# A graph layer on one core: in 13 of 128 edge blocks the last 128 source rows are fetched one by one by SyncE

## The chip, the cores and the metric

The kernel runs on one core of one Trainium2 chip. The metric is the device time of one execution in microseconds (us), median of several runs. An execution is also recorded by the hardware profiler, and all rows below come from that one recorded execution. TensorE is called PE, VectorE DVE, ScalarE ACT, GpSimd POOL and SyncE SP; PEld is the loading of weights into PE, which overlaps with its matmuls.

## The reference, cut to what matters

There are N = 8192 nodes with C = 256 numbers each, and E = 131072 edges, sorted by their destination. For every edge a message is made from the source node's row and 64 numbers of the edge; messages are summed by destination. Beside this runs attention inside groups of 32 nodes, and both results go through dense layers and a layer norm.

```python
ea = edge_attr @ w_e + b_e
msg = jax.nn.relu(x[src] + ea)
agg = jax.ops.segment_sum(msg, dst, num_segments=N)
t = x + agg
h_local = jax.nn.relu(t @ w1 + b1) @ w2 + b2
...
qkv = hd @ in_w.T + in_b
...
out = h_local + h_attn
out = out + (jax.nn.relu(out @ m_w1 + m_b1) @ m_w2 + m_b2)
...
x = _layernorm(x + ..., axis=-1)
```

The part that matters here is `x[src]`: 131072 rows of 1 KB that are picked by an index.

## The kernel before, in words

**Blocks.** The edges are cut into 128 blocks of 1024. In a block an edge has a place (h, j, partition) with h of 4, j of 2 and 128 partitions, so a block's source rows fill a tile `xs` of 128 partitions by 8 rows of 256 numbers (8 KB in each partition). `gather(b)` (lines 131 to 143) fills it with eight indirect DMAs on POOL (line 138), each with 128 indices, one row for each partition. The indices of the first two blocks come from `srcd`, later ones from `srci`. The rows come from `x` in the first 20 blocks (`NX`) and later from `xb`, a copy of `x` in DRAM to which the bias `b_e` has been added. `xs` has five buffers: the gather of block b can start when DVE has read the buffer of block b - 5. A gather is put into the program two blocks ahead of its use, but since POOL does little else, it runs as early as the buffers let it.

**A block's steps.** `load_edges(b)` (line 151) loads the block's 256 KB of edge numbers on SP's queue into one of two buffers `ea`. `edge_transpose` (line 162, DVE) turns it to `eaT` and thereby frees `ea`; the next load waits for that. `edge_products` (line 181, PE) multiplies `eaT` by `we` into two PSUM tiles `pe`; in the first 20 blocks a matmul with `sel` and `be` adds the bias (line 175). `edge_messages` adds `pe` and `xs` on DVE in two halves (line 201), and ACT applies the relu (line 202). `edge_sums` (line 221, PE) sums the messages within windows, ACT copies the sums out, `edge_place` (line 239, PE) places them among the nodes, and DVE adds them to the node tile `xT` (line 249). When all blocks of a chunk of 512 nodes are placed, the chunk's dense layers (line 496) may run.

**Order of the work.** PE's order is fixed when the program is made. Up to block 104 (`TAIL`) a loop goes through pairs of blocks and lets `work.run` put so many microseconds of attention and dense work ("fill") between the steps of a pair, by a fixed allowance. From block 104 on a planner takes over. It keeps a clock `t` and a table `came`, in which the rows of block i are due at 11.5 + 10.06 (i + 1) us; it starts at `came[102]` + 24, places a block's messages no earlier than `came`, and puts fill into the gaps as long as there is any that may run. In this part each block's messages also stand behind the newest addition to `xT` in DVE's queue. The last piece of fill is the dense work of the last 128 nodes, which needs the last block.

**SP's queue** carries the loads of `ea` and of node tiles (`xn`, line 255), the copies for `xb` (lines 566 and 572), and the output (line 549). The queue is in order: what stands behind a waiting DMA waits too. The program gives every SP DMA one of eight semaphores in turn, and each one waits until the DMA eight before it has landed.

Of the kernel before, what the change touches and what calls it, by code (L numbers as in the profile page):

```python
# [9 lines left out]
FP = mybir.dt.float32  # L10
I32 = mybir.dt.int32
# [7 lines left out]
P = 128  # L19
N, C, E, ED, H, NPG = 8192, 256, 131072, 64, 4, 32  # L20
DH = C // H
KC = C // P
BE = 1024
NB = E // BE
NH = 4
WN = P // NH
TJ = BE // NH // P
TB = NH * TJ
QR = 32
# [7 lines left out]
TN = CH // P  # L37
# [6 lines left out]
TE = 8  # L44
RS = 1.0 / (1.0 + 1e-5) ** 0.5
LN_EPS = 1e-5
REST = -1.0


# [4 lines left out]
def gnn_kernel(ctx: ExitStack, tc: tile.TileContext, x, src, dst, edge_attr, w, out):  # L54
# [30 lines left out]
    agg = dram.tile([AGG_ROWS, C], FP, name="agg")  # L85

    srci = const.tile([P, NB, TB], I32, name="srci")
    rel = const.tile([P, NB, TB], FP, name="rel")
    wrow = const.tile([P, NB], FP, name="wrow")
    width = const.tile([1, 1], I32, name="width")  # L90
    we = const.tile([P, ED // QR, C], FP, name="we")
    be = const.tile([P, C], FP, name="be")
    w1 = const.tile([P, KC, C], FP, name="w1")
    w2 = const.tile([P, KC, C], FP, name="w2")
    mw1 = const.tile([P, KC, 2 * C], FP, name="mw1")
# [32 lines left out]
        return pps.tile([P, 2, CH], FP, name="pe", tag="pe", bufs=2)  # L128


    xs_of = {}

    def gather(b):
        xs = epool.tile([P, NH, TJ, C], FP, name="xs", tag="xs", bufs=5)
        for h in range(NH):
            for j in range(TJ):
                idx = srcd[:, b * NH + h, j : j + 1] if b < ND else srci[:, b, h * TJ + j : h * TJ + j + 1]
                nc.gpsimd.indirect_dma_start(  # L138
                    out=xs[:, h, j, :],
                    out_offset=None,  # L140
                    in_=x if b < NX else xb[:, :],
                    in_offset=bass.IndirectOffsetOnAxis(ap=idx, axis=0),
                )
        xs_of[b] = xs
# [3 lines left out]
    def load_edges(b):  # L148

        ea = ea_of[b] = epool.tile([P, BE // P * ED], FP, name="ea", tag="ea", bufs=2)  # L150
        nc.sync.dma_start(ea, edge_attr[b * BE : (b + 1) * BE, :].rearrange("(p q) d -> p (q d)", p=P))

    gather(0)
    gather(1)
# [7 lines left out]
        nc.vector.transpose(eaT, ea.rearrange("p (m t d) -> p t m d", m=EQ, d=QR))  # L162


    pe_of, msg_of, oh_of, newest = {}, {}, {}, {}

    def edge_products(b):

        eaT = eaT_of.pop(b).rearrange("p t m r -> p t (m r)")
        pes = [bank2().rearrange("p i (j c) -> p i j c", j=TJ) for _ in range(2)]  # L170
        pe_of[b, 0], pe_of[b, 2] = pes
        quarter = [slice(h * QR, (h + 1) * QR) for h in range(NH)]
        if b < NX:
            for h, rows in enumerate(quarter):
                nc.tensor.matmul(  # L175
                    pes[h // 2][:, h % 2], sel[rows, :], be[rows, None, :].to_broadcast([QR, TJ, C]), start=True, stop=False, skip_group_check=True
                )
        for j in range(TJ):
            for i in range(ED // QR):
                for h, rows in enumerate(quarter):  # L180
                    nc.tensor.matmul(  # L181
                        pes[h // 2][:, h % 2, j, :], eaT[rows, j * ED // QR + i, :], we[rows, i, :],
                        start=(b >= NX and i == 0), stop=(i == 1), skip_group_check=True,
                    )

    def next_edges(b):
        if b < NB:
            edge_transpose(b)
        if b + 2 < NB:
            load_edges(b + 2)  # L190

    def edge_messages(b):

        xs = xs_of.pop(b)
        msg = msg_of[b] = epool.tile([P, NH, TJ, C], FP, name="msg", tag="msg", bufs=3)
        n = 2 if b < NB - 1 else 1
        for h in range(0, NH, 2):
            pe = pe_of.pop((b, h))
            for u in range(0, 2, n):
                hs = slice(h + u, h + u + n)  # L200
                nc.vector.tensor_add(msg[:, hs], pe[:, u : u + n], xs[:, hs])  # L201
                nc.scalar.activation(msg[:, hs], msg[:, hs], AF.Relu)  # L202

    def edge_hot(b):
# [52 lines left out]
    with tc.tile_pool(name="setup", bufs=1) as sp:  # L257
# [7 lines left out]
        for h in range(NH):  # L265
            nc.sync.dma_start(we[h * QR : (h + 1) * QR], w["w_e"].rearrange("(i d) c -> d i c", d=QR))
        load_edges(1)
        nc.sync.dma_start(be, w["b_e"][None, :].to_broadcast([P, C]))
        nc.sync.dma_start(dsti_r, dst.rearrange("(s e) -> s e", s=NB))
        in_r = npool.tile([P, 3 * KC, C], FP, name="in_r", tag="m1")  # L270
        out_r = npool.tile([P, KC, C], FP, name="out_r", tag="vn")
# [9 lines left out]
        for h in range(NH):  # L281
            nc.vector.tensor_copy(
                srcf[:, h * TJ : (h + 1) * TJ],
                srci_r[:, h * BE // NH : (h + 1) * BE // NH].rearrange("s (r m j) -> s j m r", r=QR, m=EQ),
            )
        for h in range(NH):
            ps = bank()[:, : TJ * NB].rearrange("p (j s) -> p j s", j=TJ)
            for j in range(TJ):
                nc.tensor.transpose(ps[:, j, :], srcf[:, h * TJ + j].rearrange("s m r -> s (m r)"), ident)
            nc.vector.tensor_copy(srci[:, :, h * TJ : (h + 1) * TJ].rearrange("p s j -> p j s"), ps)  # L290
# [277 lines left out]
    def copy_store(i):  # L568
        for _, c, n in steps[i] if 0 <= i < len(steps) else []:
            xp = xp_of.pop(c)  # L570
            nc.vector.tensor_add(xp, xp, be[:, None, :].to_broadcast([P, n * TN, C]))
            nc.sync.dma_start(rows(xb, c, n), xp)

    class Work:
# [64 lines left out]
    with tc.manual_schedule(engines={PE}):  # L639
# [70 lines left out]
            b += 2  # L710
        work.calm = True

        came = [11.5 + 10.06 * (i + 1) for i in range(NB)]
        t, p, m, s, l = came[b - 2] + 24, b, b, b - 2, b - 2
        added = dict((i, came[i] + 2.0) for i in range(b))
        summed_at, bank_free = {}, t
# [168 lines left out]
```

## Time and profile before

| | |
|---|---|
| median of 3 runs | 1327.83 us (1325.05 to 1328.84) |
| the profiled execution | 1328.6 us, of which its span is 1326.8 us |
| PE busy | 1210.8 us (91%), granted clock 0.961 on average |
| POOL busy | 981.7 us (74%), 1024 gathers |
| DVE busy | 784.8 us (59%) |
| ACT busy | 587.8 us (44%) |
| HBM traffic | 155 GB/s over the span |

The span lies 1.8 us under the execution's own time, and that execution lies 0.8 us above the median. Busy shares are averages over all stages. POOL's share needs care: a gather is recorded with about 0.95 us and followed by 0.30 us in which the next one is issued, and this pattern goes on without a break, so that a POOL which is 74% busy has in fact no time left. An idle time is put down to the event that came last; `issue` means that none is seen.

### The profile page before, as it was taken

Reading aid. Unit: us, or ns where it says so; the run is one execution under the profiler, and the core shown is the slowest. Engines: PE = TensorE matmul, PEld = TensorE weight load, DVE = VectorE, ACT = ScalarE, POOL = GpSimd, SP = SyncE. Lnnn points to the kernel's source line nnn. Section 1 sums busy time; section 2 is a strip of 40 time slices with the busy share of each in tenths; the row PEclk is TensorE's granted clock in tenths of the full one; section 3 lists DMA queues with packets and bytes.
Section 4 is the critical chain, followed back from the end, with each engine's and each line's share of the span. In section 5 each row is a group of like instructions: output and inputs, shape, how many; then the busy total and the mean of one; then the engine's idle time right before and its main releaser. Section 6 shows DMA issues by size and latency. Waiting matters only on the chain.

```text
span 1326.8 us, 24218 instructions
## 1 busy us (share of the span) xinstructions
PE 1210.8 (91%) x9683; PEld 738.3 (56%) x9683; DVE 784.8 (59%) x1347; ACT 587.8 (44%) x842; POOL 981.7 (74%) x1032
## 2 busy tenths in 40 slices
PE   5998899999999889898998989899999999989887
PEld 3565555555555556555564555555555565545655
DVE  6566655747565555745566474655558475565654
ACT  2534344444545354453535444444454545344433
POOL 7777777777777777777777777777777777777770
PEclk7998999999998899999899989999999999989999
DMA  8877554545454544545454454544545445444541
GB/s 284 274 253 272 189 174 136 167 130 160 137 169 128 162 129 131 160 136 163 129 146 143 135 160 131 160 139 129 162 137 170 129 139 160 131 143 130 161 122 32
DMA packets 92754, 207.10 MB, mean 156 GB/s; under 512 B 20798, under 2 KB 39644, under 8 KB 91868
## 3 DMA queue, kind: packets, MB, share of 16 engines
q0 software_dynamic: 49152, 134.28, 34.6%
q1 hardware_dynamic: 42908, 71.20, 16.3%
q8 instruction: 78, 1.28, 0.4%
q14 instruction: 40, 0.33, 0.1%
q10 hardware_dynamic: 576, 0.00, 0.0%
HBM read 188.64 MB, written 16.78 MB: 155 GB/s over the span
## 4 chain that ended last, share of the span: by engine, by line
PE 34%; POOL 30%; issue 16%; DVE 10%; DMA 6%; ACT 4%; SPq 1%; DVEq 0%; ACTq 0%; POOLq 0%
POOL xs L138 30%; PE at L496 10%; PE pe L181 8%; DMA xs<-xb,srci 4%; DVE msg L201 4%; PE at L399 4%; PE pw L221 3%; PE l L239 2%; PE at L477 2%; PE at L413 1%; ACT pr L440 1%; DVE eaT L162 1%; PE pe L175 1%; ACT msg L202 1%; PE at L465 1%
## 5 line engine op out<-in xcount | busy, mean ns | idle before, releaser
L138 POOL DMA_INDIRECT xs<-xb,srci x864 | 821.4, 951 | 263.1 <-issue 250.1
L202 ACT ACTIVATE msg<-msg 128x1024 f32<-128x1024 f32 (+1 forms) x258 | 270.0, 1050 | 443.2 <-DVE msg L201 440.3
L201 DVE TENSOR_TENSOR msg<-pe,xs 128x1024 f32<-128x1024 f32 (+1 forms) x258 | 305.0, 1196 | 157.3 <-PE pe L181 121.1
L181 PE MATMUL pe<-we,eaT 32*128 32x256 f32 x4096 | 297.8, 409 | 29.3 <-DVE msg L201 26.5
L181 PEld LDWEIGHTS pe<-we,eaT 32*128 32x128 f32 x4096 | 225.7, 197 | 122.2 <-issue 68.6
L138 POOL DMA_INDIRECT xs<-in_x_dram,srci x144 | 143.2, 995 | 43.9 <-issue 41.7
L162 DVE STREAM_TRANSPOSE eaT<-ea 128x512 f32<-128x512 f32 x128 | 90.2, 704 | 103.7 <-PE pe L181 98.3
L221 PE MATMUL pw<-msg,oh 128*32 128x256 f32 x2048 | 128.6, 386 | 1.6 <-DVE xT L249 1.6
L496 PE MATMUL at<-hA,mw 128*128 128x512 f32 (+2 forms) x304 | 122.6, 534 | 4.0 <-DVE hA L506 3.9
L496 PE MATMUL at<-m,mw 128*128 128x512 f32 (+2 forms) x304 | 119.4, 533 | 7.0 <-ACT m L512 6.5
L399 PE MATMUL at<-xT,inT 128*128 128x512 f32 x256 | 120.8, 599 | 0.3 <-ACT xT L389 0.2
L239 PE MATMUL l<-oh,ws 128*128 128x160 f32 x512 | 93.5, 323 | 4.6 <-ACT ws L227 3.6
L221 PEld LDWEIGHTS pw<-msg,oh 128*32 128x32 f32 x2048 | 59.2, 110 | 63.6 <-issue 24.5
L239 PEld LDWEIGHTS l<-oh,ws 128*128 128x128 f32 x512 | 76.4, 198 | 31.5 <-issue 23.5
L496 PE MATMUL at<-xT,w 128*128 128x512 f32 (+2 forms) x152 | 68.8, 586 | 23.9 <-DVE xT L249 22.9
L496 PEld LDWEIGHTS at<-m,mw 128*128 128x128 f32 x304 | 54.1, 191 | 57.5 <-issue 44.2
L496 PEld LDWEIGHTS at<-hA,mw 128*128 128x128 f32 x304 | 52.9, 190 | 53.5 <-issue 39.7
L399 PEld LDWEIGHTS at<-xT,inT 128*128 128x128 f32 x256 | 46.7, 190 | 54.3 <-issue 47.8
L496 PE MATMUL at<-h,w 128*128 128x512 f32 (+2 forms) x152 | 62.8, 537 | 2.8 <-ACT h L503 2.7
L521 DVE SCALAR_TENSOR_TENSOR zT<-at,s,zT 128x512 f32<-128x512 f32 (+2 forms) x38 | 25.3, 666 | 66.8 <-PE at L496 66.2
L477 PE MATMUL at<-oT,outT 128*128 128x512 f32 x128 | 62.2, 613 | 1.9 <-ACT oT L472 1.9
L413 PE MATMUL at<-inT,xT 128*128 128x256 f32 x256 | 60.7, 384 | 2.8 <-ACT qk L402 2.8
(107 smaller groups left out, 1143.9 us busy)
## 6 DMA issues: line engine op xcount, KB each, us to landing
ea<-in_edge_attr_dram SPq DMA_DIRECT2D x128, 256.0 KB
xs<-xb,srci POOLq DMA_INDIRECT x864
xn<-in_x_dram SPq DMA_DIRECT2D x16, 512.0 KB
out_dram<-y SPq DMA_DIRECT2D x14, 512.0 KB
xp<-in_x_dram SPq DMA_DIRECT2D x10, 512.0 KB
xb<-xp SPq DMA_DIRECT2D x10, 512.0 KB
xp<-in_x_dram SPq DMA_DIRECT2D x3, 1024.0 KB
xb<-xp SPq DMA_DIRECT2D x3, 1024.0 KB
```

What stands on the lines that cost most here:

```text
L138: nc.gpsimd.indirect_dma_start(out=xs[:, h, j, :], out_offset=None, in_=x if b < NX else xb[:, :], in_offset=bass.IndirectOffsetOnAxis(ap= ...
L162: nc.vector.transpose(eaT, ea.rearrange("p (m t d) -> p t m d", m=EQ, d=QR))
L181: nc.tensor.matmul(pes[h // 2][:, h % 2, j, :], eaT[rows, j * ED // QR + i, :], we[rows, i, :], start=(b >= NX and i == 0), stop=(i == 1), ...
L201: nc.vector.tensor_add(msg[:, hs], pe[:, u : u + n], xs[:, hs])
L202: nc.scalar.activation(msg[:, hs], msg[:, hs], AF.Relu)
L221: nc.tensor.matmul(pw[h * WN : (h + 1) * WN, i, :], oh[:, h * TJ + j, :], msg[:, h, j, :], start=(j == 0), stop=(j == TJ - 1), skip_group_ ...
L239: nc.tensor.matmul(l2[:, k, i * NPB : i * NPB + WB], ws[:, i, k * P : (k + 1) * P], oh2[:, i, :], start=(i == 0 and k == 0), stop=(i == la ...
L399: nc.tensor.matmul(ps, inT[:, k, o * P : (o + 1) * P], xT[:, k, :], start=(k == 0), stop=(k == KC - 1))
L413: nc.tensor.matmul(ps[:, (t - t0) * C : (t - t0 + 1) * C], xT[:, k, t * P : (t + 1) * P], inT[:, k, 2 * C :], start=(k == 0), stop=(k == K ...
L477: nc.tensor.matmul(ps, outT[:, k, o * P : (o + 1) * P], oT[:, k, :], start=(k == 0), stop=(k == KC - 1))
L496: nc.tensor.matmul(ps, wt[:, k, o * P : (o + 1) * P], act[:, k, :], start=(k == 0), stop=(k == nk - 1))
L521: nc.vector.scalar_tensor_tensor(zT[:, o, :], layer(mw2, 2 * KC, o, m1), s3[:, o : o + 1], zT[:, o, :], op0=ALU.mult, op1=ALU.add)
```

## The change

Blocks 31, 39, ..., 127 (13 blocks, `R0` = 31, `RB` = 8) gather only seven of their eight index columns. Their last 128 rows go into a tile `xr` of 1 KB in each partition (two buffers). They are fetched in eight portions of 16, one portion in each of the eight blocks ahead: `load_rows(b)` is called at the end of `next_edges`, right after the load of `ea`; SP loads 16 indices from the tile `srcr` into registers, and then issues 16 DMAs of one row each, with the address from a register. `tc.issue_after` keeps them behind the newest load of `ea`. The tile `srcr` is a copy of the indices of the last column, made once at the start. Where a block has such rows, the second addition of `edge_messages` is split in two, 768 and 256 numbers wide, the second one reading `xr`.

Room for this is made in SBUF: `xs` has four buffers, not five. The bias tile `be` grows from 1 KB to 2 KB in each partition, and is loaded already repeated. The planner's table `came` counts 1.2575 us for a gather (eight of them are 10.06 us) and leaves out those that are gone.

```diff
+RB = 8
+R0 = 31
...
+    srcr = const.tile([P, P], I32, name="srcr")
...
-    be = const.tile([P, C], FP, name="be")
+    be = const.tile([P, TJ, C], FP, name="be")
...
+    by_row = range(R0, NB, RB)
+
+    def load_rows(b):
+
+        q = next((q for q in by_row if b < q), None)
+        if q is None or b < q - RB:
+            return
+        if q not in xr_of:
+            xr_of[q] = epool.tile([P, C], FP, name="xr", tag="xr", bufs=2)
+        p0, p1 = ((b - q + RB + k) * P // RB for k in range(2))
+        _, rows = nc.values_load_multi_w_load_instructions(
+            srcr[q : q + 1, p0:p1], engines=(mybir.EngineType.SP,), min_val=0, max_val=N - 1,
+            skip_runtime_bounds_check_because="indices of nodes",
+        )
+        with tc.issue_after(newest["ea"]):
+            for p, row in enumerate(rows, p0):
+                nc.sync.dma_start(xr_of[q][p : p + 1, :], (x if q < NX else xb)[ds(row, 1), :])
...
-        xs = epool.tile([P, NH, TJ, C], FP, name="xs", tag="xs", bufs=5)
+        xs = epool.tile([P, NH, TJ, C], FP, name="xs", tag="xs", bufs=4)
         for h in range(NH):
-            for j in range(TJ):
+            for j in range(TJ - (b in by_row and h == NH - 1)):
...
-        nc.sync.dma_start(ea, edge_attr[b * BE : (b + 1) * BE, :].rearrange("(p q) d -> p (q d)", p=P))
+        newest["ea"] = nc.sync.dma_start(ea, edge_attr[b * BE : (b + 1) * BE, :].rearrange("(p q) d -> p (q d)", p=P)).ins
...
             load_edges(b + 2)
+        load_rows(b)
...
-                nc.vector.tensor_add(msg[:, hs], pe[:, u : u + n], xs[:, hs])
+                by = (msg[:, hs], pe[:, u : u + n], xs[:, hs])
+                if b in by_row and hs.stop == NH:
+                    a, p, g = (t.rearrange("p h j c -> p (h j) c") for t in by)
+                    k = a.shape[1] - 1
+                    nc.vector.tensor_add(a[:, :k], p[:, :k], g[:, :k])
+                    nc.vector.tensor_add(a[:, k], p[:, k], xr_of.pop(b))
+                else:
+                    nc.vector.tensor_add(*by)
...
-        nc.sync.dma_start(be, w["b_e"][None, :].to_broadcast([P, C]))
+        nc.sync.dma_start(be, w["b_e"][None, None, :].to_broadcast([P, TJ, C]))
...
+        nc.vector.tensor_copy(srcr, srcf[:, TB - 1].rearrange("s m r -> s (m r)"))
...
-        came = [11.5 + 10.06 * (i + 1) for i in range(NB)]
+        came = [11.5 + 1.2575 * ((i + 1) * TB - sum(q <= i for q in by_row)) for i in range(NB)]
```

More of the change, by code (lines that the diff above doesn't have):

```diff
@@ L128, in bank2 @@
         return pps.tile([P, 2, CH], FP, name="pe", tag="pe", bufs=2)
-    xs_of = {}
+    xs_of, newest = {}, {}
+    xr_of = {}
+    by_row = range(R0, NB, RB)
[13 more added lines that the diff above has]
+                nc.sync.dma_start(xr_of[q][p : p + 1, :], (x if q < NX else xb)[ds(row, 1), :])
     def gather(b):
-        xs = epool.tile([P, NH, TJ, C], FP, name="xs", tag="xs", bufs=5)
+        xs = epool.tile([P, NH, TJ, C], FP, name="xs", tag="xs", bufs=4)
         for h in range(NH):
-            for j in range(TJ):
+            for j in range(TJ - (b in by_row and h == NH - 1)):
                 idx = srcd[:, b * NH + h, j : j + 1] if b < ND else srci[:, b, h * TJ + j : h * TJ + j + 1]
@@ L162, in edge_transpose @@
         nc.vector.transpose(eaT, ea.rearrange("p (m t d) -> p t m d", m=EQ, d=QR))
-    pe_of, msg_of, oh_of, newest = {}, {}, {}, {}
+    pe_of, msg_of, oh_of = {}, {}, {}
     def edge_products(b):
@@ L175, in edge_products @@
                 nc.tensor.matmul(
-                    pes[h // 2][:, h % 2], sel[rows, :], be[rows, None, :].to_broadcast([QR, TJ, C]), start=True, stop=False, skip_group_check=True
+                    pes[h // 2][:, h % 2], sel[rows, :], be[rows], start=True, stop=False, skip_group_check=True
                 )
@@ L570, in copy_store @@
             xp = xp_of.pop(c)
-            nc.vector.tensor_add(xp, xp, be[:, None, :].to_broadcast([P, n * TN, C]))
+            nc.vector.tensor_add(xp, xp, be[:, 0:1, :].to_broadcast([P, n * TN, C]))
             nc.sync.dma_start(rows(xb, c, n), xp)
```

## The prediction

> **What bounds the kernel now.** I read the page's engine shares and its chain first, then the waits, then POOL's and DVE's timelines side by side. The page's chain names POOL:
>
> ```profile
> PE 34%; POOL 30%; issue 16%; DVE 10%; DMA 6%; ACT 4%; SPq 1%; DVEq 0%; ACTq 0%; POOLq 0%
> L138 POOL DMA_INDIRECT xs<-xb,srci x864 | 821.4, 951 | 263.1 <-issue 250.1
> ```
>
> The gathers are one unbroken row: POOL's timeline shows 0.95 us each and 0.30 us to the next, the same at 452 us and at 1224 us:
>
> ```profile
> 452.42 0.95 POOL L138 DMA_INDIRECT xs<-xb,srci  x1 [0.30 <-issue]
> ...
> 734.91 0.94 POOL L138 DMA_INDIRECT xs<-xb,srci  x1 [0.30 <-issue]
> ...
> 1225.30 0.95 POOL L138 DMA_INDIRECT xs<-xb,srci  x1 [0.30 <-issue]
> ...
> 1295.42 0.94 POOL L138 DMA_INDIRECT xs<-xb,srci  x1 [0.30 <-issue]
> ```
>
> 1024 of 1.25 us are 1280 us, and the last one ends at 1296.4. So POOL has no slack, and it never waited for a buffer. But does anyone wait for POOL? The chain cannot tell, because it steps back along POOL's own queue. I laid each block's two additions (L201) beside its eight gathers (POOL's timeline counted in eights). From block 46 on, the first addition begins 3.8 to 19.0 us after the block's last gather has ended, in blocks 60 to 103 mostly 10 to 15. A gather lands some 2.7 to 3.7 us after its end (chain rows "694.11 2.74 DMA xs" and "755.20 3.67"). Among blocks 26 to 126 I find DVE idle for a gather in three places alone, blocks 35, 37 and 43, with 0.89, 0.17 and 1.88 us. DVE's timeline, two of them, and block 120, whose last gather is the 1225.30 row above (ended 1226.25):
>
> ```profile
> 374.89 1.23 DVE L201 TENSOR_TENSOR msg<-pe,xs 128x1024 f32<-128x1024 f32 x1 [0.89 <-DMA xs<-xb,srci]
> ...
> 456.51 1.23 DVE L201 TENSOR_TENSOR msg<-pe,xs 128x1024 f32<-128x1024 f32 x1 [1.88 <-DMA xs<-xb,srci]
> ...
> 1237.81 1.22 DVE L201 TENSOR_TENSOR msg<-pe,xs 128x1024 f32<-128x1024 f32 x1
> ```
>
> Who does end DVE's waits is in the list of waits: PE's products, not gathers (other rows put down to gathers, as at 820.7, come 18 us after the gather in question had ended, so their cause was another):
>
> ```profile
> DVE msg L201 <- PE pe L181: 121.1, 49, 9.0
> ...
> DVE msg L201 <- DMA xs<-xb,srci: 14.3, 8, 4.7
> ...
> SPq L151 <- DVE eaT L162: 962.1, 117, 21.7
> ```
>
> So PE, 91% busy in an order written out beforehand, sets the pace; POOL runs at nearly the same pace, ahead of it. SP mostly waits.
>
> **The change part by part.**
>
> *Gathers removed.* 13 x 1.25 = 16.3 us of POOL's row. On the path lies only what somebody waited for: 0.89 + 0.17 + 1.88 = 2.9 us. Blocks 31 and 39 bring gathers 1.25 us forward before block 35, and 2.5 before block 43, more than these waits. PE felt the largest: it was idle for 4.21 us before 457.95 (a dense layer waiting for `xT`, which stood behind that addition). Bounds: 0 (the next wait takes its place) to 16.3. I take -2.9, by the DVE rows. In blocks 46 to 103 nothing is taken: PE's order is the same there and its fill allowance is too, so the cover is PE's own work; if the cover were gone, the full 16.3 would show.
>
> *The tail, from block 104.* The planner's due times shrink by 1.2575 us at 103, 111, 119 and 127, so from its start to the last block by 5.0 us: fill of that size leaves the early tail and stands later. Whether that is a gain depends on idle PE later. Between 1200 and 1300 us PE was busy 86.38 of 100 us, so 13.6 idle, mostly around blocks with no fill (products waiting for the additions to free PSUM). All 5.0 may fall into it, or none. I take -4, nearer to the idle side since 13.6 is well over 5.0.
>
> *Four buffers.* The gather of block b now waits for the addition of block b - 4. In the profile the smallest distance between that addition's end and the gather's start is 9.0 us (the addition of block 68 ends at 725.9, the gather of block 72 starts at 734.9), 9.4 at block 80, 9.3 at block 100, else mostly 12 to 25. POOL's advance by then is 7.5, 8.8 and 11.3 us: it is stopped for about 2 us at block 100 if PE is unmoved. Nothing waits for these gathers, which are still some 20 us ahead of use, so the cost is 0; the cover is that lead.
>
> *SP.* In 104 block steps (8 for each of 13 blocks) come one index load, 16 register steps and 16 DMAs. Price of a row's DMA: this trace has issues of small transfers at the start (`vec_r`), 0.23 to 0.30 us each:
>
> ```profile
> 7.08 0.60 SPq L275 DMA_DIRECT2D vec_r<-in_L_gnn_b_dram  x2
> 7.86 0.23 SPq L275 DMA_DIRECT2D vec_r<-in_L_gnn_bn_g_dram  x1
> ...
> 14.12 0.40 SPq L276 DMA_DIRECT2D in_r<-in_L_gnn_in_w_dram  x1
> ```
>
> Lower bound 0.23 us; upper bound with waits for the eighth before, 12 issues from 7.08 to 14.12, or 0.59 each (DMA then 89% busy, now 45 to 55%). A register step is not in the trace: between SP's shortest event (0.017 us) and one more issue (0.23). I take 0.30 for the row, nearest to the plain issue. The index load: the nearest is the wait at the program's end for such a load (L763, up to 0.5 us). Together 16 x 0.30 + 0.5 + 0.33 for `ea` = 5.6 us of each 10.06; if the second eight rows wait for the first to land (2.7 to 3.7 us), 6 to 7. SP is moved past nothing that can't bear it: `ea` loads were issued 10.0 us (block 108) or, mostly, 16 to 25 us ahead of their transposes; `xn` of chunk 13 was issued 10.8 us ahead of PE's use, the tightest, and a batch in front of it takes at most some 5 us of that. Cost 0, upper bound in the rival below.
>
> The Trainium skill's page "DMA: Bandwidth & Descriptors", "Anatomy of one DMA — SWDGE (gpsimd) path", gives about 2.0 us fixed for a DMA, however small. This speaks against 16 single rows, and agrees with the 2.7 us landing; with eight in flight it would make 2 x 2.0 = 4 us a batch, less than SP's issue time taken above, so the sum is the same by either. The same page's "Latency and other measured facts" puts an index load at a floor of about 0.6 us, against the 0.5 taken here; an estimate from it changes a batch by 0.1.
>
> *DMA engines.* The same 1 KB rows, 16 per block beside 1024: their bytes were gathered before. Cost 0; if all rows of a batch went to one of the 16 engines, at 0.08 us a packet (q1: 16.3% of 16 x 1326.8 us over 42908 packets) that engine gets 1.3 us more per block on top of about 5.
>
> *DVE.* 13 split additions. From the row widths (1024: 1.204 us, 512: 0.660) the fixed part is 0.12 us, plus up to seven waits of 0.02 to 0.05 for the row semaphores: at most 0.5 each, 6 us in all, DVE being 59% busy. PE was seen waiting for an addition in 43 of 256 cases, so one sixth of it, +1. Bounds 0 to +6.
>
> *Start.* `be` loads 256 KB, not 128, while DMA runs at 298 GB/s: 0.4 us, and a copy of the indices on DVE, 0.2 by a row of like width. Bounds 0 to +0.6; +0.5.
>
> Sum: -2.9 - 4 + 0 + 0 + 1 + 0.5 = -5.4 us against the profiled execution's 1328.6, so 1323.2; that execution is 0.8 above the median, so **1322.4**.
>
> **The rivals.**
>
> *POOL's row does set the time.* The chain's 30% and 16% speak for it, the 3.8 to 19 us of lead against. Then 16.3 us come off less 1.5: 1327.8 - 14.8 = 1313.0.
>
> *Hidden anyway.* The three waits are followed by others, and the tail's fill only moves: -1.4 to +1.5, so 1326 to 1329. For it: between 280 and 1320 us PE was idle for only 76 us (1040 less 964.44 busy), mostly by its own chains.
>
> *SP becomes the bound.* The place is the batch behind each `ea` load, which keeps the next load, and through it the transposes and products, behind 16 rows. It decides when a row passes (10.06 - 0.33 - 0.5 - 0.1) / 16 = 0.57 us, the 0.1 being SP's other DMAs. At the upper bound of 0.59 a block takes 10.4, so 104 x 0.3 = 31 us more: 1359; each further 0.1 us costs 166. For it: the start's 0.59, and the untried register form. Against: the plain 0.23 to 0.33.
>
> *The new tail order makes PE wait.* A dense layer that stands too early waits for `xT`, as at 457.95 (4.21 us). Two such waits more, and the idle part not filled: 2 x 4.2 + 1.5 - 2.9 = +7, so 1335. It decides from one such wait more. Against: the plan keeps its own rules.
>
> **How the numbers follow.** Forecast 0.50 (1316 to 1323.8); POOL's row 0.10; hidden 0.17; SP 0.12; tail order 0.11. About 0.3%, 4 us, is what a measurement tells from no change. Faster 0.50 + 0.10 = 0.60, same 0.17, slower 0.12 + 0.11 = 0.23. The range 1313 to 1337 leaves out SP's 0.12, about half of POOL's 0.10, and little else.
>
> **What would show it.** Right: POOL's gathers end 14 to 16 us earlier, at about 1281 to 1283; additions lag them by more than 10 us in the tail; no addition waits for a gather in blocks 35, 37, 43; PE's idle between 1200 and the end falls by some 4 us; SP's rows take 0.25 to 0.35 us and its waits for `eaT` stay several us long. Wrong: DVE waiting for `ea` or `xr`, SP's row over 0.5 us, or a saving near 16 us, which would say that the lead of the gathers was not slack.

## The result, and the profile after

The changed kernel takes 1316.85 us (median of 6 runs, 1311.77 to 1319.88), the kernel before 1327.96 us (median of 6, 1325.05 to 1328.90): a ratio of 0.9916 with a 95% interval of 0.9891 to 0.9940, or 11.1 us less (8.0 to 14.5). The forecast was 1322.4, or 5.4 less. The profiled execution took 1319.52 us, with a span of 1317.7.

Two things have to be known to read the numbers below. First, a run's time moves with the clock that the throttle grants to PE, and this clock differs from run to run (0.960 to 0.976). So besides the medians I give each kernel's time at the clock 0.968, read from a straight line through all of its own runs. Second, in two of the four sessions of experiments this program was far slower on the whole, the kernel before too (2075.01 and 2030.11 us, granted clock about 0.83), so that the times of each of these two are compared within it alone.

| kernel | median us (runs) | ratio to before, 95% interval | us against before | us at clock 0.968, against before's 1326.7 |
|---|---|---|---|---|
| changed kernel | 1316.85 (6) | 0.9916 (0.9891 to 0.9940) | -11.1 | 1317.9, -8.8 |
| rows, old planner table | 1325.31 (12) | 0.9985 (0.9969 to 1.0002) | -2.0 | 1324.8, -1.9 |
| new planner table alone | 1320.58 (6) | 0.9951 (0.9933 to 0.9969) | -6.5 | 1321.6, -5.1 |
| four buffers alone | 1327.14 (12) | 1.0001 (0.9988 to 1.0014) | 0.1 | 1327.2, 0.5 |
| rows in blocks 31 and 39 alone | 1322.84 (12) | 0.9965 (0.9952 to 0.9978) | -4.6 | 1323.6, -3.1 |
| changed, rows left out | 1314.23 (4) | 0.9904 (0.9888 to 0.9921) | -12.7 | 1314.7, -12.1 |
| changed, small bias, earlier table | 1311.77 (4) | 0.9883 (0.9866 to 0.9899) | -15.5 | 1314.0, -12.7 |

The fourth column is the ratio's distance from 1 times 1328; the ratio is not quite that of the two medians. The last column says how far a kernel lies from the kernel before at the same clock.

Of the page after, the busy row, the chain and the group of the gathers:

```profile
PE 1203.5 (91%) x9683; PEld 734.1 (56%) x9683; DVE 784.9 (60%) x1361; ACT 587.5 (45%) x842; POOL 972.6 (74%) x1019
...
PE 48%; POOL 16%; DVE 11%; issue 10%; DMA 9%; ACT 5%; SPq 1%; DVEq 0%; POOLq 0%; ACTq 0%
...
L159 POOL DMA_INDIRECT xs<-xb,srci x851 | 812.3, 954 | 259.6 <-issue 245.0
```

PE's busy share is as before, but its busy time is 7.3 us less (1210.8 to 1203.5). This is hardly the change's doing: the profile of four buffers alone, a kernel that is no faster by its median, has 1204.3 (granted clock 0.967, where the profile before has 0.961 and the one after 0.966). POOL still runs without a break, 0.95 us and 0.30 us in turn, but its part of the chain has halved from 30% to 16%. The shares cannot say whether that is the gain: they walk along POOL's row as long as there is one.

The list of waits after. The columns are who waited for whom, the total in us, the number of waits and the longest:

```profile
DVE msg L230 <- PE pe L202: 123.7, 50, 10.4
...
DVE msg L230 <- DMA xs<-xb,srci: 8.9, 5, 3.1
...
PE at L418 <- DMA xn<-in_x_dram: 1.6, 1, 1.6
```

The additions wait for PE's products as before (50 waits, 123.7 us against 49, 121.1), and less for gathers (8.9 us against 14.3). Most of the waits put down to gathers are not real, before and after: laid beside the gathers from block 26 on, the additions of these waits began either 1.9 to 3.9 us after the end of the last gather that they need, or 7.7 us and more after it, and in the second case the gather had long landed. By this measure 2.9 us of the 14.3 are real, in the three blocks that the prediction names, and 1.3 us of the 8.9: 0.21 us in block 37 and 1.07 us in block 45 (at 474.95 us). One matmul group has waited 1.6 us for a node tile `xn`. SP's waits for `eaT`, in the same list for SP alone, are a quarter of the old 962.1 us:

```profile
SPq L172 <- DVE eaT L183: 241.3, 53, 13.0
```

The timelines of the changed kernel show the places where the prediction looked. Columns: start in us, length, engine, line, operation, and in brackets the idle time ahead of it with what ended it.

```profile
395.86 1.23 DVE L230 TENSOR_TENSOR msg<-pe,xs 128x1024 f32<-128x1024 f32 x1 [0.21 <-DMA xs<-xb,srci]
...
455.48 1.98 PE L526 MATMUL at<-xT,w 128*128 128x512 f32 x4 [2.08 <-DVE xT L278]
...
1258.71 0.70 PE L202 MATMUL pe<-we,eaT 32*128 32x256 f32 x4 [1.06 <-DVE msg L230]
1260.43 2.00 PE L202 MATMUL pe<-we,eaT 32*128 32x256 f32 x28 [1.03 <-DVE msg L230]
1266.50 4.91 PE L202 MATMUL pe<-we,eaT 32*128 32x256 f32 x32 [1.72 <-DVE msg L230]
...
1283.29 0.95 POOL L159 DMA_INDIRECT xs<-xb,srci  x1 [0.30 <-issue]
...
1294.92 1.88 DVE L230 TENSOR_TENSOR msg<-pe,xs 128x512 f32<-128x512 f32 x3
```

The dense layer in block 43 waits 2.08 us for `xT` where it waited 4.21. The last gather ends at 1284.2, 12.1 us earlier than before, and the last block's additions begin 10.7 us after it. In the tail the products' waits for additions are fewer. These are the waits of more than 1 us of the kernel before between 1180 and 1310 us:

```profile
1221.78 2.00 PE L181 MATMUL pe<-we,eaT 32*128 32x256 f32 x28 [1.44 <-DVE msg L201]
1239.08 0.70 PE L181 MATMUL pe<-we,eaT 32*128 32x256 f32 x4 [1.91 <-DVE msg L201]
1240.93 3.51 PE L181 MATMUL pe<-we,eaT 32*128 32x256 f32 x28 [1.15 <-DVE msg L201]
1268.12 0.70 PE L181 MATMUL pe<-we,eaT 32*128 32x256 f32 x4 [1.06 <-DVE msg L201]
1269.85 2.00 PE L181 MATMUL pe<-we,eaT 32*128 32x256 f32 x28 [1.03 <-DVE msg L201]
1275.92 0.70 PE L181 MATMUL pe<-we,eaT 32*128 32x256 f32 x4 [1.72 <-DVE msg L201]
```

Six have become three. Added over all of the tail (from 1055 us), PE's waits for additions were 9.6 us before and are 5.1 after.

How far each block is from the kernel before (start of its first addition, after minus before, from the two DVE timelines; a minus is ahead): +2.0 us at block 0, +1.8 in blocks 8 to 32, -0.5 at 43, -4.7 at 44, -3.3 at 103 and -8.4 at 127. So there is a loss at the start, a step at block 44, and a gain of 5.1 us in the tail. Between 45 and 103 it moves about between -6.8 and -3.3, while PE's work is the same; the profile of four buffers alone, whose median is no faster, goes from -0.3 to -7.2 there, so one profile cannot place a gain in this stretch.

PE's idle time by stretch (gaps of more than 0.1 us in which neither a matmul nor a weight load runs) does not depend on the clock as much:

| us | 0 to 280 | 280 to 480 | 480 to 1055 | from 1055 |
|---|---|---|---|---|
| before | 26.8 | 10.7 | 39.0 | 25.5 |
| changed kernel | 28.0 | 8.0 | 42.8 | 21.0 |
| rows, old table | 28.7 | 7.5 | 41.0 | 26.2 |
| new table alone | 24.7 | 11.0 | 41.0 | 20.9 |
| four buffers alone | 26.7 | 11.0 | 40.9 | 26.4 |
| rows in 31 and 39 alone | 29.2 | 7.4 | 40.9 | 25.5 |
| changed, rows left out | 26.8 | 9.4 | 42.4 | 19.5 |
| changed, small bias, earlier table | 26.5 | 7.8 | 41.3 | 18.1 |

Added up, the gaps are 102.0 us before and 99.8 after, only 2.2 less, while the spans differ by 9.1: the start and the middle stretch lost 5.0 us of the 7.2 that the other two won, and nearly all the rest of the 9.1 is PE's shorter busy time, which came with the run. A fairer pair is the profile of four buffers alone, at nearly the clock of the changed kernel's: gaps of 105.0 against 99.8 us, spans of 1323.2 against 1317.7, so 5.2 us in gaps and 5.5 in all. The size of the gain is thus less sure than its direction: 5.5 us by this one pair, 8.8 at equal clock by the lines, 11.1 by the ratio.

### The profile page after: what moved, and what is told of

Its sections match the earlier page's. It is cut to its first block, busy times and chain, and to the rows that moved or that the text cites. A ratio compares the mean times of both kernels' runs of the same rounds, so it can differ in the third digit from the quotient of the medians.

```text
span 1317.7 us, 29360 instructions
## 1 busy us (share of the span) xinstructions
PE 1203.5 (91%) x9683; PEld 734.1 (56%) x9683; DVE 784.9 (60%) x1361; ACT 587.5 (45%) x842; POOL 972.6 (74%) x1019
## 4 chain that ended last, share of the span: by engine, by line
PE 48%; POOL 16%; DVE 11%; issue 10%; DMA 9%; ACT 5%; SPq 1%; DVEq 0%; POOLq 0%; ACTq 0%
POOL xs L159 16%; PE at L526 14%; PE pe L202 11%; PE at L429 6%; DMA xs<-xb,srci 5%; PE pw L250 5%; DVE msg L230 4%; PE l L268 3%; PE at L507 3%; PE at L443 3%; ACT msg L231 1%; DVE eaT L183 1%; DMA xs<-in_x_dram,srci 1%; ACT pr L470 1%; PE pe L196 1%
## 5 line engine op out<-in xcount | busy, mean ns | idle before, releaser
L159 POOL DMA_INDIRECT xs<-xb,srci x851 | 812.3, 954 | 259.6 <-issue 245.0
L230 DVE TENSOR_TENSOR msg<-pe,xs 128x1024 f32<-128x1024 f32 (+1 forms) x245 | 290.0, 1199 | 156.0 <-PE pe L202 123.7
L202 PE MATMUL pe<-we,eaT 32*128 32x256 f32 x4096 | 294.8, 407 | 26.2 <-DVE msg L230 23.5
L268 PE MATMUL l<-oh,ws 128*128 128x160 f32 x512 | 89.6, 314 | 2.6 <-ACT ws L256 1.6
L268 PEld LDWEIGHTS l<-oh,ws 128*128 128x128 f32 x512 | 73.0, 191 | 28.8 <-issue 23.7
L526 PE MATMUL at<-xT,w 128*128 128x512 f32 (+2 forms) x152 | 68.2, 581 | 21.6 <-DVE xT L278 20.9
L432 ACT ACTIVATE qk<-at,vec 128x512 f32<-128x512 f32 x64 | 43.4, 683 | 47.7 <-PE at L429 46.8
```

The costliest lines, as they stand in the source:

```text
L159: nc.gpsimd.indirect_dma_start(out=xs[:, h, j, :], out_offset=None, in_=x if b < NX else xb[:, :], in_offset=bass.IndirectOffsetOnAxis(ap= ...
L202: nc.tensor.matmul(pes[h // 2][:, h % 2, j, :], eaT[rows, j * ED // QR + i, :], we[rows, i, :], start=(b >= NX and i == 0), stop=(i == 1), ...
L230: nc.vector.tensor_add(*by)
L268: nc.tensor.matmul(l2[:, k, i * NPB : i * NPB + WB], ws[:, i, k * P : (k + 1) * P], oh2[:, i, :], start=(i == 0 and k == 0), stop=(i == la ...
L432: nc.scalar.activation(qk[:, o, :], ps, AF.Identity, bias=v_("in_b", o))
L526: nc.tensor.matmul(ps, wt[:, k, o * P : (o + 1) * P], act[:, k, :], start=(k == 0), stop=(k == nk - 1))
```

## The experiments

The theory after the result: the gain has two places, the waits for gathers before block 44, which need rows in blocks 31 and 39 alone, and the tail, where it comes from the planner's table. The rival: POOL's row sets the time and each gather that is gone pays.

### The rows without the new table

```diff
-        came = [11.5 + 1.2575 * ((i + 1) * TB - sum(q <= i for q in by_row)) for i in range(NB)]
+        came = [11.5 + 10.06 * (i + 1) for i in range(NB)]
```

> The changed kernel with the planner's old table of due times (10.06 us for every block); rows, four buffers and the wider bias tile stay. Theory (PE's written order sets the time): PE stays some 3 to 6 us ahead of the kernel before up to block 103, as in the changed kernel, but the gain of about 5 us after block 104 is gone: 1321 to 1324 us. Rival (POOL's row of gathers sets the time, its last gather now ends 12 us earlier): nothing is lost against the changed kernel, about 1317 us.

Measured: 1325.31 us, 0.9985 (0.9969 to 1.0002). This is slower than the theory had it (1321 to 1324), and far from the rival's 1317. In its profile PE is 7.0 us ahead at block 103 and still 7.2 ahead at block 127, although the gathers come 11 us earlier at the first and 15 us earlier at the second. The last rows of gathers and additions:

```profile
1280.37 0.94 POOL L159 DMA_INDIRECT xs<-xb,srci  x1 [0.30 <-issue]
...
1296.10 1.28 DVE L230 TENSOR_TENSOR msg<-pe,xs 128x512 f32<-128x512 f32 x2
```

In the tail the lead of the gathers has grown to 14.8 us and nothing else: thirteen gathers less, at 16.3 us in all, are worth 2.0 us (between a gain of 4.1 and a loss of 0.3), after what SP's rows cost (see the run without them below). POOL's row as a whole did not set the time in the kernel before, which would have given 14.8 us.

### The new table without the rows

```diff
+        by_row = range(31, NB, 8)
-        came = [11.5 + 10.06 * (i + 1) for i in range(NB)]
+        came = [11.5 + 1.2575 * ((i + 1) * TB - sum(q <= i for q in by_row)) for i in range(NB)]
```

This edit is made in the kernel before: all 1024 gathers, five buffers, no row fetched.

> The kernel before with the new table of due times alone; all eight gathers of each block and five buffers stay. Theory: the tail is written in the new order, which is worth 3 to 5 us by itself, since additions there came 4 to 11 us after the last gather anyway: 1323 to 1325 us, the same up to block 103. Rival: the planner now counts on rows that come up to 16 us later than it thinks, PE stands behind them: no gain, 1328 us or more.

Measured: 1320.58 us, 0.9951 (0.9933 to 0.9969), more than the theory gave. More than half of the whole gain comes from one line that tells the planner of gathers that are faster than they are. In its profile PE goes from 1.3 us ahead at block 103 to 7.3 at block 127. But there the gathers are at their limit: the additions of blocks 112, 124 and 127 begin 0.1, -0.2 and 0.0 us after the block's last gather has ended (a half can be added before the last gather). Three second additions wait for a gather, in blocks 112, 124 and 125, for 1.36, 1.02 and 0.54 us; they begin 1.9 to 2.7 us after the last gather that they need. The last gather ends within 0.01 us of the last block's first addition:

```profile
1148.04 1.23 DVE L201 TENSOR_TENSOR msg<-pe,xs 128x1024 f32<-128x1024 f32 x1 [1.36 <-DMA xs<-xb,srci]
...
1277.89 1.23 DVE L201 TENSOR_TENSOR msg<-pe,xs 128x1024 f32<-128x1024 f32 x1 [0.54 <-DMA xs<-xb,srci]
...
1295.04 0.95 POOL L138 DMA_INDIRECT xs<-xb,srci  x1 [0.30 <-issue]
...
1295.98 2.63 DVE L201 TENSOR_TENSOR msg<-pe,xs 128x512 f32<-128x512 f32 x4
```

So the new table spends the lead of the gathers down to nothing. Whether this costs time here is not shown: PE's gaps from 1055 us are 20.9 us, as in the changed kernel (21.0), and PE gains 6.0 us from block 103 to 127, where the changed kernel gains 5.1. The runs' times hint at a cost when PE is faster. At a granted clock of 0.965 to 0.967 this kernel takes 1320.32 and 1322.69 us and the changed one (at 0.966) 1319.52 and 1319.88. At 0.970 to 0.974 it takes 1324.03, 1320.32, 1320.84 and 1319.46, while the changed kernel (0.971 to 0.973) takes 1314.50, 1315.13 and 1311.77. These are few runs from two sessions that scatter by several us at one clock, so this is a hint and no more.

### Four buffers alone

```diff
-        xs = epool.tile([P, NH, TJ, C], FP, name="xs", tag="xs", bufs=5)
+        xs = epool.tile([P, NH, TJ, C], FP, name="xs", tag="xs", bufs=4)
```

> The kernel before with four buffers of gathered rows in place of five, nothing else. Theory: the gather of a block never waits for the addition four blocks before (smallest distance 9.0 us in the profile): within 1 us of before, 1327 to 1329 us. Rival (the fifth buffer is what keeps POOL unbroken): POOL's last gather ends later than 1296.4 us, and the time rises by as much.

Measured: 1327.14 us, 1.0001 (0.9988 to 1.0014): the fifth buffer was worth nothing. From block 20 on, a gather starts at least 11.3 us after the addition that frees its buffer, and in the changed kernel at least 4.3 us (block 100). POOL was never stopped, not even for the 2 us that the prediction allowed for.

This profile shows one thing more. PE ran at a higher clock than in the profile before (0.967 against 0.961) and was 6.8 us ahead of it at block 103, with all gathers and the old table. There the lead of the gathers was used up (0.3 us), and second additions of six blocks from 103 to 112 waited for gathers, 5.8 us in all. Two of them:

```profile
1128.66 1.23 DVE L201 TENSOR_TENSOR msg<-pe,xs 128x1024 f32<-128x1024 f32 x1 [1.74 <-DMA xs<-xb,srci]
...
1138.90 1.23 DVE L201 TENSOR_TENSOR msg<-pe,xs 128x1024 f32<-128x1024 f32 x1 [1.42 <-DMA xs<-xb,srci]
```

They began 2.3 and 2.5 us after the last gather that they need had ended. By block 127 PE was only 3.7 us ahead. In the run of rows with the old table PE was as far ahead at block 103 (7.0 us), nobody waited, and it kept 7.2. So with the old table too the gathers have little slack in the tail: in the profile before nobody waits for them there, in a faster run somebody does. POOL's row is a limit close behind PE's order, though not the one that set the time in the profile that the prediction read.

### Rows in blocks 31 and 39 alone

```diff
-    by_row = range(R0, NB, RB)
+    by_row = (31, 39)
```

The table falls by two gathers ahead of the tail and not in it, so that the tail is planned as before.

> The changed kernel with rows in blocks 31 and 39 alone (the table of due times with them). Theory: these two take away the waits for gathers at blocks 35, 37 and 43, PE is about 4.5 us ahead from block 44 on and keeps part of it, and the tail is planned as before, less the tail's gain: 1321 to 1325 us. Rival (POOL's row): 2 of 13 gathers, so 2.5 us: 1325.5 us, and the additions at block 44 only 2.5 us earlier.

Measured: 1322.84 us, 0.9965 (0.9952 to 0.9978). In its profile block 43 is 0.9 us late and block 44 3.3 us early; the dense layer's wait is the changed kernel's:

```profile
456.85 1.99 PE L526 MATMUL at<-xT,w 128*128 128x512 f32 x4 [2.08 <-DVE xT L278]
```

In the tail it stays 7.0 us ahead from block 100 to 127. Two blocks of thirteen give 4.6 us (2.9 to 6.4), and the table alone 6.5 (4.1 to 8.9): together the 11.1 that the whole change gives. The other eleven blocks add nothing to that sum, and with the old table thirteen blocks gave no more than two (2.0 us). Whether the eleven help the new table is not measured: no run has the new table with rows in blocks 31 and 39 alone.

### The change without the fetching of rows

```diff
-            xr_of[q] = epool.tile([P, C], FP, name="xr", tag="xr", bufs=2)
+            xr_of[q] = xz
...
-        _, rows = nc.values_load_multi_w_load_instructions(
-            srcr[q : q + 1, p0:p1], engines=(mybir.EngineType.SP,), min_val=0, max_val=N - 1,
-            skip_runtime_bounds_check_because="indices of nodes",
-        )
-        with tc.issue_after(newest["ea"]):
-            for p, row in enumerate(rows, p0):
-                nc.sync.dma_start(xr_of[q][p : p + 1, :], (x if q < NX else xb)[ds(row, 1), :])
```

`xz` is a tile of zeros, made once. The section on five more runs has this kernel once more.

> The changed kernel without the 104 index loads and the 1664 row fetches; the last column of the 13 blocks is added from a tile of zeros, so the source rows of those 128 edges a block are left out of the result. Theory: SP's batches of 8.2 us a block hold up nothing, since the ea loads came at least 8.1 us before their transposes and PE waited 1.55 us for node tiles once: the ratio to the kernel before is that of the changed kernel, 0.9916, less 0 to 1.5 us: 0.9900 to 0.9920 (1315 to 1318 us where the kernel before takes 1328). Rival, the rows cost time by late loads of node tiles, by their DMAs beside the gathers (some gathers were longer than before), or by the additions that wait for them: 0.985 to 0.988 (1308 to 1312 us).

Measured: 1314.23 us, 0.9904 (0.9888 to 0.9921), where the changed kernel has 0.9916 (0.9891 to 0.9940): the rows cost 1.6 us by the ratios and 3.2 by the lines at clock 0.968, and the intervals overlap, so that a cost of nothing is not excluded. A large one is, and no wait for an `xr` is in the changed kernel's list. What SP does for the rows, in the changed kernel (minimum, median and maximum in ns):

```profile
L152 SPq FUSED_REGOPS  x1664: 37/37/51, 244.9 to 1274.2; - x185
L152 SPq MOVE xr<-xb x1664: 29/29/38, 245.0 to 1274.3; - x185
L152 SPq DMA_DIRECT2D xr<-xb x1664: 224/228/303, 245.1 to 1274.4; - x185
```

```profile
L146 SPq TENSOR_LOAD <-srcr x104: 1163/1194/3311, 243.6 to 1265.9; - x104
```

The three instructions of a row add up to 0.294 us, but with the time between them SP takes 0.41 us for each row, for the first eight of a batch as for the second eight. No row waits for the one eight before it: such a wait is not in SP's list. SP's queue in the changed kernel's timeline, where a batch of 16 rows has 6.4 to 6.8 us and the load of `ea` is issued right behind it:

```profile
961.15 6.75 SPq L152 DMA_DIRECT2D xr<-xb  x16
968.49 0.36 SPq L172 DMA_DIRECT2D ea<-in_edge_attr_dram  x1
970.25 6.43 SPq L152 DMA_DIRECT2D xr<-xb  x16
976.92 0.36 SPq L172 DMA_DIRECT2D ea<-in_edge_attr_dram  x1
```

From one load of `ea` to the next are 8.4 us here, and 9.2 to the one after: SP is full in this stretch. In 59 of 102 blocks the load was issued more than 0.3 us (up to 9.0) after its buffer was free. But it was still at least 8.1 us ahead of the transposes that read it, and none of them waited.

### A row every fourth block

```diff
-RB = 8
+RB = 4
```

Now 25 blocks have rows, and SP issues 32 of them in each block. The kernel before takes 2075.01 us beside it.

> The changed kernel with rows in every fourth block from 31 on (25 blocks, 32 rows in each step). Theory: SP becomes the bound. By the changed kernel's trace a step is 1.39 us for the index load, 0.41 us for each row and 0.36 for the edge load: 14.9 us for a block of 10, so about 100 x 4.9 = 490 us slower, 1800 us; if SP is held by issue alone (0.29 us a row), 10.9 us and 90 us slower, 1410 us. Rival (two buffers of edges and the waits hide it): 1310 to 1317 us.

Measured: 2546.04 us, 1.231 (1.2252 to 1.2368), 471 us more, where the theory had 490. Its waits show the prediction's rival "SP becomes the bound" at work:

```profile
PE at L418 <- DMA xn<-in_x_dram: 436.6, 11, 50.1
...
DVE msg L228 <- DMA xr<-xb: 126.0, 11, 19.3
```

A batch of 32 took 12.9 to 28.1 us, 17.6 on average, so 0.55 us a row where the theory had 0.41, and the index load 2.19 us on average where it had 1.39; that the sum came out near the forecast is in part luck. PE feels it most by the node tiles, which stand in the same queue: 11 waits of 436.6 us in all. So the mechanism is real, and 32 rows a block are too many; where between 16 and 32 it begins was not measured.

### A small bias tile and an earlier table

```diff
-    be = const.tile([P, TJ, C], FP, name="be")
+    be = const.tile([P, C], FP, name="be")
...
+        came = [c - 0.4 * max(i - TAIL + 1, 0) for i, c in enumerate(came)]
```

(and `be` loaded once and read by broadcast again, as before).

> The changed kernel with the bias tile of the kernel before (1 KB in each partition) and with the planner's due times brought forward by 0.4 us more for each block from 104 on. Theory: the wide bias costs what the first addition lost at the start, 1.8 to 2.0 us, and the tail follows the planner's table as long as gathers end before the additions; in the profile of the changed kernel they ended 9 to 17 us before. The table moves 9.6 us by block 127, so the tail has room for nearly all of it, and the gain is 2 us from the bias and some 4 to 7 us from the tail: ratio to the kernel before 0.984 to 0.988 (1307 to 1312 us where the kernel before takes 1328). Rival, the fill is used up: then the moved blocks leave PE idle elsewhere in the tail, only the bias counts, 0.990 (1315 us). Rival, the start's 2 us are hidden by the time of block 44, and the tail is at its limit: as the changed kernel, 0.9916 (1317 us).

Measured: 1311.77 us, 0.9883 (0.9866 to 0.9899), the fastest kernel of this study, just short of the theory's 0.984 to 0.988. PE's wait for the bias at the start, in the kernel before, in the changed kernel, and in this one:

```profile
11.37 2.09 PE L175 MATMUL pe<-be,sel 32*128 32x512 f32 x8 [1.10 <-DMA be<-in_L_gnn_b_e_dram]
```

```profile
12.94 2.09 PE L196 MATMUL pe<-be,sel 32*128 32x512 f32 x8 [2.02 <-DMA be<-in_L_gnn_b_e_dram]
```

```profile
11.48 2.09 PE L196 MATMUL pe<-be,sel 32*128 32x512 f32 x8 [0.61 <-DMA be<-in_L_gnn_b_e_dram]
```

Its first addition is 0.1 us ahead of the kernel before's, where the changed kernel's is 2.0 late. In the tail it goes from 2.9 us ahead (block 103) to 13.8 (block 127): 10.9 us, where the changed kernel gained 5.1. The table moves 5.0 + 9.6 = 14.6 us there, so three quarters became time. The lead of the gathers over the additions is still 8.9 us at the end. How the gain over the changed kernel (3.9 us at clock 0.968) divides between the two edits is not settled by the times: in the run without rows, which has the wide bias, the 2.5 us lost at block 0 were gone by block 16.

### Five more runs, where the kernel before takes 2030 to 2075 us

Beside a kernel before of 2075.01 us the small bias alone, the rows left out and the earlier table alone ran, by the diffs above:

> The changed kernel with the bias tile as before (1 KB in each partition, loaded once, repeated by the matmul's access pattern). Theory: the wider load delays the start, where the changed kernel's first additions come 1.8 to 2 us later than before; that shift goes and stays gone to the end: additions of blocks 8 to 32 within 0.7 us of the kernel before, 1314.5 to 1316.5 us. Rival (the start's delay is made up later, since POOL's row or the load of indices waits anyway): 1317 us as the changed kernel.

> The changed kernel without the index loads and the 1664 row DMAs: in the 13 blocks the last column is added from a tile of zeros, so the source rows of those 128 edges are left out of the messages. POOL's gathers, the plan and the split additions stay. Theory: SP's rows are hidden but for node tiles (xn) that now come late for chunks 13 to 15 (PE waits 1.55 us for one): 1 to 2 us faster than the changed kernel, 1315 to 1317 us. Rival (rows on SP or on the DMA engines slow the gathers or the edge loads): 5 us or more faster, at most 1312 us.

> The changed kernel with due times that come 0.4 us closer for each block from 104 on (9.6 us at the last block in all); rows and gathers unchanged. Theory (the tail is limited by its written order, and gathers end 10 us before use): the tail shortens further, by up to 5 us where PE has idle time left (21 us after 1055): 1311 to 1316 us. Rival (POOL's row): the planner now counts on rows before they land, additions wait for gathers, no gain: 1317 us or more.

Measured: 2078.04 us, 1.0012 (0.9983 to 1.0042) with the small bias; 2048.29 us, 0.9878 (0.9833 to 0.9923) with the rows left out; 2072.29 us, 0.9964 (0.9929 to 1.0000) with the earlier table. Beside a kernel before of 2030.11 us the small bias and the earlier table were run again:

> The changed kernel with the bias tile as before, again, to be compared where the kernel before takes 1328 us. Theory: the start's delay of about 2 us goes, and 1 to 2 us of it are left at the end: 1314.5 to 1316.5 us, ratio to before 0.990 to 0.991, and additions of blocks 8 to 32 within 0.7 us of the kernel before. Rival (made up later): as the changed kernel, 1317 us.

> The changed kernel with due times that come 0.4 us closer for each block from 104 on, again, to be compared where the kernel before takes 1328 us. Theory (the tail is limited by its written order and not by gathers): faster than the changed kernel by 1 to 5 us, 1312 to 1316 us, with additions still at least 3 us after the last gather's end. Rival (POOL's row): additions wait for gathers in the tail, 1317 us or more.

Measured: 2058.24 us, 1.0155 (1.0089 to 1.0220), and 2055.68 us, 1.0142 (1.0081 to 1.0203). Here the kernels that fetch rows are level with the kernel before or slower. The kernel with the rows left out is 24 us faster than with the earlier table and 30 us faster than with the small bias; the changed kernel itself was not run there, so what SP's rows cost here is not measured cleanly, though it looks like more than the few us found above. POOL's gathers wait for the additions that free their buffers in all five (484 to 504 us in their lists of waits; in the eight profiles of 1313 to 1327 us no such wait is longer than 0.3 us), so four buffers bind here; with five no profile was taken. None of the expectations, which count on a kernel before of 1328 us, is decided by these runs.

## Why the prediction was right, and where it was wrong

The direction, the two places of the gain and the range (1313 to 1337) were right; the gain was sized at half: 5.4 us against 11.1, or against 8.8 at equal clock. About 2.3 us of the difference thus lies in the runs' clocks and not in the kernel. The one pair of profiles at nearly equal clock gives 5.5.

- **Gather waits, -2.9: right in kind, and about right in size.** The real waits for gathers near the start fell from 2.9 to 1.3 us: 35 and 43 wait no more and 37 waits 0.21, but block 45 now waits 1.07, as the bound "the next wait takes its place" allowed. PE's gaps between 280 and 480 us fell by 2.7 us, by 3.2, 3.3 and 2.9 in the three other kernels that fetch rows, by 1.3 with the rows left out, and not at all in the two that gather everything. Rows in blocks 31 and 39 alone took off 4.6 us (2.9 to 6.4), start included.
- **The tail, -4 with -5.0 as the bound: right in its mechanism, too small in size.** PE's gaps from 1055 us fell by 4.5 us, and it was the named ones, products that wait for additions (9.6 to 5.1 us). But the table alone measured 6.5 us (4.1 to 8.9), or 5.1 at equal clock, so the value to take was the bound, 5.0, and not a part of it. The earlier table shows that the room was larger still.
- **"POOL runs ahead": true for the profile that was read, not for every run.** In the profile before, no addition of the tail waits for a gather. With four buffers alone and PE 6.8 us further ahead, six do, and with the new table and all gathers the lead falls to nothing. The sum took each term as if it stood alone. Rows with the old table give 2.0 us and the table without rows 6.5, in sum 8.5 of 11.1 (7.0 of 8.8 at equal clock). The rest may appear only with both; but it lies within the intervals, and with the 4.6 us of blocks 31 and 39 in place of the 2.0 nothing is left over. This stays open.
- **Four buffers, 0: right**, by the run of it alone; the lead at block 100 was larger than assumed.
- **SP, 0: the cost about right, the price of a row wrong.** The three instructions of a row have 0.294 us (37 + 29 + 228 ns), but SP spends 0.41 us on a row (16 rows in 6.6 us on average), not the 0.30 taken; the waits for the eighth row before, which were the upper bound, did not occur. The index load takes 1.19 us in the median and 1.39 in the mean, not 0.5. A batch with its index load has 8.2 us, some 8.5 with the load of `ea`, and not 5.6. The Trainium skill's "DMA: Bandwidth & Descriptors", "Latency and other measured facts", has a floor of some 0.6 us for such a load; the load here is twice that. What saved the forecast was slack in `ea`, at least 8.1 us. The point at which SP decides lies nearer than forecast: with a load of 1.39 us a row may take (10.06 - 0.36 - 1.39 - 0.1) / 16 = 0.51 us, not 0.57, and it takes 0.41.
- **The split additions, +1: not contradicted.** Halves of 0.918 and 0.407 us replace one of 1.19 to 1.23, some 0.12 us more, and 40 waits on semaphores have 0.05 each: 13 x 0.12 + 40 x 0.05 = 3.6 us on DVE, of which the one sixth assumed is 0.6. The sixth itself is too high: the 43 cases are 23 waits of PE and 20 of its weight loads, and 15 of the latter fall within 1 us of one of the former. No run took the split away.
- **The start, +0.5 with +0.6 as the bound: wrong.** The first addition came 2.0 us late, and 1.7 to 2.5 us in the three other kernels with the wide bias; PE waited 2.0 to 3.3 us for `be` in these four, and 0.6 to 1.1 in the four with the small one. The bytes of the wide bias were counted as 0.4 us; why it comes later than that by more than 1 us stays open. How much of the delay is left at the end is not shown either: at block 32 the changed kernel is 1.8 us late, but the table alone, whose start is unchanged, is 2.2 early there.
- **The signs.** POOL's gathers end 12.1 us earlier, where 14 to 16 were said; other runs with the same gathers gave 15.0 to 17.1. The additions of the tail lag the gathers by 8.8 to 20.0 us, not by more than 10 throughout. SP's waits for `eaT` are 13.0 us at most and several us on average, as said. The rival "POOL's row sets the time" fell with the first experiment, in its full size; "SP becomes the bound" came with twice the rows; a tail order that makes PE wait did not come.

That the forecast came as near as it did is in part luck: the tail was sized too small, and so was the start's loss, as far as it lasts, and these two errors work against each other.

## What to carry to other kernels

A queue that runs without a break takes up the chain in a profile whether or not anyone waits for it; lay its ends beside their use, and then ask again with the new order, since a lead that is slack today can be spent by the next change, or by a run in which the other engine is a little faster. A constant in a planner can be worth more than the work it describes: change it alone first. Before a difference of two profiles is put down to a change, add up the idle and the busy time of each, and look at a third profile that is no faster. A wait that is put down to a gather is real only if the gather ended shortly before.

## What the runs showed of the hardware

- Loading 16 indices from SBUF into SP's registers took 1.16 us at least and up to 3.31 (104 loads in the changed kernel).
- A 1 KB row with its address from a register took 0.41 us of SP's time, in three instructions of 37, 29 and 228 ns with some 0.12 us between them. No row waited for the one eight before it, so a row landed within some 8 x 0.41 = 3.3 us (an estimate of the most it can be).
- Additions that did wait for a gather began 1.9 to 3.9 us after the end of the last gather that they need (21 cases in six profiles). The 2.0 us of the Trainium skill's page ("DMA: Bandwidth & Descriptors", "Anatomy of one DMA — SWDGE (gpsimd) path"), fixed for a DMA issued by GpSimd, are at the lower end of this.
- Along the straight lines the kernel before becomes 5.4 us faster for 0.01 more of granted clock (37 runs), and the others 1.6 (the table alone, six runs) to 10 (the changed kernel, six runs); with so few runs each these are not told apart.
